# An LSTM's output weights loaded through the ring of the input weights, and its second block of steps fetched from inside the recurrence

## The chip, the core and the metric

The kernel runs on one core of a Trainium2 chip. Its engines are TensorE (PE in the profile; its weight loads are PEld), VectorE (DVE), ScalarE (ACT), GpSimd (POOL) and SyncE (SP, which here only issues DMAs and waits). The metric is the device time of one execution in microseconds; times before and after are medians of several runs. A "q" behind an engine's name in the profile means its instruction queue: the DMA issues and semaphore waits that the engine itself isn't busy with.

## The reference, cut to what matters

A stack of four graph layers and four other layers runs over 625 nodes with 512 features. The change lies in the sixth of these eight phases, a switching LSTM: the 625 nodes are 625 steps of one sequence, and at every step the argmax of four logits picks which of four sets of weights computes the gates.

```python
def step(carry, x_t):
    h, c = carry
    sel_in = jnp.concatenate([h, c, x_t], axis=-1)
    logits = sel_in @ W_sel.T + b_sel
    onehot = jax.nn.one_hot(jnp.argmax(logits, axis=-1), Sx, dtype=x_t.dtype)
    g_all = (jnp.einsum('bi,sgi->bsg', x_t, W_ih) + jnp.einsum('bh,sgh->bsg', h, W_hh)
             + b_ih + b_hh)
    g = jnp.einsum('bsg,bs->bg', g_all, onehot)
    h2, c2 = _lstm_activate(g, c)
    return ((h2, c2), h2)
```

`_lstm_activate` splits the gates into i, f, g and o and takes `c2 = sigmoid(f)*c + sigmoid(i)*tanh(g)` and `h2 = sigmoid(o)*tanh(c2)`. The result is added to the layer's input, and a normalized graph convolution follows.

## The kernel before, in words

Each phase is a function; `L2_ffn` is the LSTM. Everything outside the recurrence is written with a tile framework: a pool is a piece of on-chip memory that is taken from the left or the right end and given back when it is closed, a tile is a piece of a pool, and the framework works out all semaphores and the order on each engine's queue from what reads and writes what. A queue is worked off in order.

`L2_ffn` has two stages. In the first, the *input projection*, no step depends on another. Four experts times four gates make 16 turns (`turn = e * 4 + g`). Each turn takes a 512x512 block of W_ih, loaded by `C.weight` (line 91) into a ring of three 1 MB places (pool `weights`, at the right end), multiplies it with `xT`, the input laid out by feature (64 matmuls at line 1561, two halves of the nodes by four row blocks by four chunks of the sum), evacuates with a bias on ACT (line 1565) or DVE (lines 1568 and 1570) into a tile `gt`, and writes that to the DRAM tensor `gx` (line 1573), once for each half of the nodes. Two `gt` tiles take turns. In between, in the first twelve turns, half-megabyte pieces of W_hh come in as `raw` (issued by `load_whh`, line 1471; pool `e_raw`, two places, at the right end) and are split by ACT and DVE (`split`, lines 1478 to 1482) into three bf16 parts each, the tiles `wp`, which stay in memory. They are the recurrent weights of the gates i, f and g.

The second stage is the *recurrence*, 625 steps in which every engine runs its own hand-written program with its own semaphores (`tile_critical`, line 1674). Nothing in it begins before all that it uses is there; the framework makes SP wait for everything ahead of it and lets all engines go together. The fourth gate's recurrent weights stay in float32: four tiles `wo`, 8 KB a partition and 1 MB each, loaded through line 1471 after the projection's pools are closed; their pool `e2` lies in the room that `xT`, the `gt` tiles and their neighbours had. Behind `e2` lie the recurrence's own small tiles (pool `e_state`), among them two buffers `gxb` for 25 steps' worth of gx each (800 KB) and two `xsb` of the selection's input. `fetch(b)` loads one block of 25 steps into them (lines 1668 and 1670): `fetch(0)` and `fetch(1)` are issued ahead of the recurrence, and from block 2 on SP's own program in the recurrence issues them when DVE and ACT say that a buffer is free (line 1681); DVE and ACT wait for a block's arrival at its first step. The history `hist` of all h lies at the right end, where the ring of weights was.

In a step, TensorE multiplies the guessed expert's `wp` with h (line 1719) and `wo` (line 1748), DVE transposes and sums, ACT takes the functions. A matmul into `spare` (line 1760) opens each step's program on TensorE. The first instruction that DVE runs in the recurrence is the memset at line 1807.

Of the kernel before, what the change touches and what calls it, by code (L numbers as in the profile page):

```python
# [15 lines left out]
F32 = mybir.dt.float32  # L16
# [5 lines left out]
AF = mybir.ActivationFunctionType  # L22
# [6 lines left out]
N, D, P, NT = 625, 512, 125, 5  # L29
KC = D // 128  # L30
# [9 lines left out]
BLOCKS = N // STEPS  # L40
# [8 lines left out]
class Ctx:  # L49
# [21 lines left out]


    def open_mid(self, side):
        self.outer, self.inner = (self.stack.enter_context(ExitStack()) for _ in range(2))
        pool = lambda of, name, bufs: of.enter_context(self.tc.tile_pool(name=name + side, bufs=bufs, side=side))
        self.weights = pool(self.outer, "weights", 3)
        self.small = pool(self.outer, "small", 2)
        mid = pool(self.inner, "mid", 1)
        self.iota = mid.tile([128, N], F32, name="iota")
        self.nc.gpsimd.iota(self.iota, pattern=[[1, N]], base=0, channel_multiplier=0,  # L80
                            allow_small_or_imprecise_dtypes=True)
        self.x = mid.tile([P, NT, D], F32, name="x")
# [1359 lines left out]
def L2_ffn(C):  # L1442
# [6 lines left out]
    nc, tc, I = C.nc, C.tc, C.ins  # L1449
    S = 4  # L1450
    W = lambda name: I["L2_ffn_" + name]
    ORDER = (0, 1, 3, 2)
# [4 lines left out]
    with ExitStack() as st:  # L1457
        E = st.enter_context
# [3 lines left out]
        st1 = E(ExitStack())  # L1462
        pool = st1.enter_context(tc.tile_pool(name="e", bufs=1))
# [4 lines left out]
        def load_whh(dst, e, g, s0, n):  # L1468

            q = ORDER[g]  # L1470
            nc.sync.dma_start(dst, W("WhhT")[:, e, s0:s0 + n, q * D:(q + 1) * D])
# [12 lines left out]
        halves = [(e, g, s0) for e in range(S) for g in range(3) for s0 in (0, 2)]  # L1484

        with ExitStack() as st2:
            E2 = st2.enter_context
# [6 lines left out]
                C.normed(C.x)  # L1494
                C.feature_major(ps, xT, C.x)
            C.inner.close()
            st4 = E2(ExitStack())
            praw = st4.enter_context(tc.tile_pool(name="e_raw", bufs=2, side="right"))
            pgt = E2(tc.tile_pool(name="e_gt", bufs=2))
            st3 = E2(ExitStack())  # L1500
# [8 lines left out]
            b = praw.tile([64, 2, 128], F32, name="raw")  # L1509
# [34 lines left out]

            st3.close()
            ps = E2(tc.tile_pool(name="e_ps2", bufs=4, space=PSUM))
            for e in range(S):
                for g, q in enumerate(ORDER):
                    w = C.weight(W("WihT")[e, :, q * 512:(q + 1) * 512].rearrange("(k p) n -> p k n", p=128), KC)
                    turn = e * 4 + g  # L1550
                    pieces = []
                    for half in halves[turn * 2:turn * 2 + 2]:
                        raw = praw.tile([128, 2, D], F32, name="raw")
                        load_whh(raw, *half, 2)
                        pieces += [(raw, *half, s) for s in range(2)]
                    for n0, n in HALVES:
                        gt = pgt.tile([128, HALVES[0][1], 4], F32, name="gt")
                        for s in range(4):
                            pg = ps.tile([128, 512], F32, name="pg")
                            for k in range(KC):  # L1560
                                nc.tensor.matmul(pg[:, :n], w[:, k, s * 128:(s + 1) * 128], xT[:, k, n0:n0 + n],  # L1561
                                                 start=k == 0, stop=k == KC - 1)
                            c = (e * 4 + q) * 4 + s
                            if s % 2:
                                nc.scalar.activation(gt[:, :n, s], pg[:, :n], AF.Identity, scale=2.0 if g == 2 else 1.0,  # L1565
                                                     bias=(bias_2 if g == 2 else bias)[:, c:c + 1])
                            elif g == 2:
                                nc.vector.tensor_scalar(gt[:, :n, s], pg[:, :n], bias[:, c:c + 1], 2.0, op0=ALU.add, op1=ALU.mult)
                            else:
                                nc.vector.tensor_scalar(gt[:, :n, s], pg[:, :n], bias[:, c:c + 1], None, op0=ALU.add)  # L1570
                            if s % 2 and pieces:
                                split(*pieces.pop(0))
                        nc.sync.dma_start(gx[e, g, :, n0 * 4:(n0 + n) * 4], gt[:, :n].rearrange("p n c -> p (n c)"))

            st4.close()
            C.outer.close()
            held = E(tc.tile_pool(name="e_hist", bufs=1, side="right"))
            hist = held.tile([128, N + 1, KC], F32, name="hist")
            x4 = held.tile([P, D], F32, name="x4")
            nc.vector.tensor_copy(x4, kept[-1])  # L1580
            kept[-1] = x4
        pool = st1.enter_context(tc.tile_pool(name="e2", bufs=1))
        wo = [pool.tile([128, KC, D], F32, name=f"wo{e}") for e in range(S)]
        for e in range(S):
            load_whh(wo[e], e, 3, 0, KC)
        state = st1.enter_context(tc.tile_pool(name="e_state", bufs=1))
        with tc.tile_pool(name="e_ps3", bufs=1, space=PSUM) as ps:
            recurrence(C, state, ps, wp, wo, wsel, gx, xs, hist)
        st1.close()
        C.open_mid("left")  # L1590
        with tc.tile_pool(name="e_ps4", bufs=3, space=PSUM) as ps:
            for t in range(NT):
                pt = ps.tile([P, D], F32, name="pt")
                for s in range(KC):
                    nc.tensor.transpose(pt[:, s * 128:(s + 1) * 128], hist[:, 1 + t * P:1 + (t + 1) * P, s], C.ident)
                if t < NT - 1:
                    nc.scalar.copy(C.x[:, t], kept[t])
                    kept[t] = C.x[:, t]
                nc.vector.tensor_add(C.x[:, t], kept[t], pt)
                C.seen(t)  # L1600


def recurrence(C, pool, ps, wp, wo, wsel, gx, xs, hist):
# [19 lines left out]
    nc, tc = C.nc, C.tc  # L1623
    S, FIRST = 4, 6
# [17 lines left out]
    th = t_([128, 4], "th")  # L1642
# [20 lines left out]
    loaded = [nc.alloc_semaphore(f"lstm_dma{i}") for i in range(2)]  # L1663
    free = [[nc.alloc_semaphore(f"lstm_free_{k}{i}") for k in ("dve", "act")] for i in range(2)]

    def fetch(b):

        return (nc.sync.dma_start(gxb[b % 2].rearrange("p a u c -> p a (u c)"),
                                  gx[:, :, :, b * STEPS * 4:(b + 1) * STEPS * 4].rearrange("s q p f -> p (s q) f")),
                nc.sync.dma_start(xsb[b % 2], xs[0:1, b * STEPS * ROW:((b + 1) * STEPS + 1) * ROW]))  # L1670

    fetch(0)
    fetch(1)
    with tc.tile_critical():
        with nc.Block() as block:

            @block.sync
            def _(sync):
                for b in range(2, BLOCKS):
                    for f in free[b % 2]:  # L1680
                        sync.wait_ge(f, b // 2)
                    for d in fetch(b):
                        d.then_inc(loaded[b % 2], 16)

# [93 lines left out]
            @block.scalar  # L1778
            def _(act):
                for n in range(N):  # L1780
                    b, u = divmod(n, STEPS)
                    if b >= 2 and u == 0:
                        act.wait_ge(loaded[b % 2], 32 * (b // 2))
                    act.wait_ge(sem["ga0"], 1).then_inc(sem["ga0"], -1)  # L1784

                    act.copy(xrow[:, :S], xsb[b % 2][:, (u + 1) * ROW:(u + 1) * ROW + S]).then_inc(sem["x"])  # L1786
                    m = act.copy(hist[:, n], hT)
                    if u == STEPS - 1 and b < BLOCKS - 2:
                        m.then_inc(free[b % 2][1])
                    act.wait_ge(sem["ga"], 1)  # L1790
                    act.activation(act4[:, 0:3].rearrange("p g s -> p (g s)"), ga, AF.Tanh, scale=0.5).then_inc(sem["ifg"])  # L1791
                    act.wait_ge(sem["ao"], 1)
                    act.activation(so, go, AF.Sigmoid).then_inc(sem["so"])  # L1793
                    act.wait_ge(sem["c"], 1)
                    act.activation(th, c2, AF.Tanh, scale=0.5).then_inc(sem["th"])

            @block.vector
            def _(dve):
# [13 lines left out]
                dve.memset(hT, 0.0).then_inc(sem["hb"])  # L1812
                index()
                for b in range(BLOCKS):
                    if b >= 2:
                        dve.wait_ge(loaded[b % 2], 32 * (b // 2))
                    gxs = gxb[b % 2].rearrange("p (e g) u c -> p e g u c", e=S)
                    with dve.Fori(0, STEPS) as u:
                        wait("ix").then_inc(sem["dx"])
# [148 lines left out]


PHASES = [graph_and_L0_gnn, L0_ffn, L1_gnn, L1_ffn, L2_gnn, L2_ffn, L3_gnn, L3_ffn]  # L1970


# [48 lines left out]
```

## Time and profile before

| | us |
|---|---|
| median of three runs | 5129.65 (5128.46 to 5135.43) |
| the profiled execution | 5125.94 |
| its span, first to last instruction | 5123.2 |
| input projection, first to last matmul at line 1561 | 1366.0 to 1637.0 |
| first matmul of the recurrence | 1660.65 |
| last step's functions on ACT end | 4754.7 |
| a step of the recurrence, most frequent length | 4.6 |
| granted TensorE clock, mean over the span | 0.971 |

All times inside the execution count from the span's start. A row of the timeline gives the start, the length, the engine, the line, the operation with what it writes and reads, how often it came in a row, and in brackets how long its engine stood idle before it and what ended that. "issue" as the cause means that the profile shows nothing that the engine waited for. A row of the waits gives the total, the count and the longest wait. The chain of waits from the last instruction doesn't lead back through the recurrence here (it holds 8% of the span), so what follows is read from queues and windows. What can be seen apart from that is how much of the time DMAs carry: 246.84 MB over the whole span, 48 GB/s on the mean.

### The profile page before, as it was taken

What the parts mean: (1) busy time and instruction counts of PE and PEld (TensorE: products, weight loads), DVE (VectorE), ACT (ScalarE), POOL (GpSimd) and SP (SyncE); (2) the same over time, 40 slices, a digit from 0 to 9 for tenths busy, and PEclk for the clock granted to TensorE, in tenths of its full rate; (3) what the DMA queues carried; (4) which work ended last, traced back from release to release, by engine and by line L of the source; (5) the groups of instructions that cost most, each with busy time, mean ns of one, the idle gap of its engine ahead of it and who ended that gap; (6) DMA issues with size and microseconds to landing.
All of it is one profiled execution on the core that took longest, in us unless ns stands there. A gap on an engine that the chain in (4) does not pass through costs nothing. (4 is left out here: it accounts for less than half of the span.)

```text
span 5123.2 us, 184391 instructions
## 1 busy us (share of the span) xinstructions
PE 4752.5 (93%) x74110; PEld 3009.7 (59%) x74110; DVE 2662.2 (52%) x13487; ACT 1127.4 (22%) x4582; POOL 152.3 (3%) x140
## 2 busy tenths in 40 slices
PE   8998988799998999999999999999999999999988
PEld 6566746555575555555555555555555555555555
DVE  7533034400441566666656566665666656556258
ACT  8443112101341111111111111111111111111136
POOL 0000012100000000000000000000000000000011
PEclk9998998799999999999999999999999999999988
DMA  1133957211354000000000000000000000000200
GB/s 39 64 109 119 318 174 243 73 52 43 115 186 144 2 11 6 6 6 7 7 6 6 7 7 6 6 6 7 7 6 7 7 7 6 6 6 0 72 13 11
DMA packets 163039, 246.84 MB, mean 48 GB/s; under 512 B 67001, under 2 KB 67374, under 8 KB 162124
## 3 DMA queue, kind: packets, MB, share of 16 engines
q1 hardware_dynamic: 144480, 221.36, 13.2%
q0 software_dynamic: 8800, 16.92, 1.1%
q10 hardware_dynamic: 9594, 6.59, 0.5%
q8 instruction: 76, 1.25, 0.1%
q14 instruction: 89, 0.73, 0.0%
HBM read 198.90 MB, written 45.91 MB: 48 GB/s over the span
## 5 line engine op out<-in xcount | busy, mean ns | idle before, releaser
L1719 PE MATMUL pa<-wp,left 128*23 128x384 bf16 x33312 | 1495.6, 327 | 136.8 <-issue 46.6
L1719 PEld LDWEIGHTS pa<-wp,left 128*23 128x23 bf16 x33312 | 805.7, 93 | 649.6 <-DVE left L1856 154.0
L1748 PE MATMUL po<-wo,left 128*1 128x128 f32 x20000 | 655.7, 273 | 0.0
L1748 PEld LDWEIGHTS po<-wo,left 128*1 128x1 f32 x20000 | 481.1, 84 | 126.2 <-issue 0.2
L1760 PE MATMUL spare<-wo,ident 128*128 128x256 f32 x1250 | 437.4, 431 | 26.6 <-issue 26.6
L1824 DVE COPY col<-gxb 128x16 f32 x625 | 114.6, 183 | 654.3 <-DVEq L1799 654.3
L1834 DVE STREAM_TRANSPOSE col<-pa 128x384 f32<-128x384 f32 x625 | 349.5, 559 | 195.1 <-PE pa L1719 195.1
L1791 ACT ACTIVATE act<-ga 128x12 f32<-128x12 f32 x625 | 132.7, 212 | 1183.6 <-DVE ga L1836 1183.6
L1786 ACT COPY xrow<-xsb 1x4 f32<-1x4 f32 x625 | 120.5, 193 | 1214.8 <-ACTq L1784 1214.8
L1760 PEld LDWEIGHTS spare<-wo,ident 128*128 128x128 f32 x1250 | 186.1, 188 | 167.1 <-issue 167.1
L1561 PE MATMUL pg<-xT,w 128*128 128x312 f32 (+1 forms) x1024 | 270.4, 426 | 0.9 <-ACT gt L1565 0.5
L1561 PEld LDWEIGHTS pg<-xT,w 128*128 128x128 f32 x1024 | 193.2, 189 | 77.7 <-DVE gt L1570 1.1
L1711 PE MATMUL lg<-wso,th 128*1 128x8 f32 x5008 | 216.2, 169 | 14.0
L1707 PE MATMUL lg<-wsel,act 128*1 128x8 f32 x5008 | 216.2, 169 | 2.7 <-DVE act L1845 1.2
L1838 DVE STREAM_TRANSPOSE col<-po 128x128 f32<-128x128 f32 x625 | 198.2, 317 | 22.8
L1711 PEld LDWEIGHTS lg<-wso,th 128*1 128x1 f32 x5008 | 147.6, 81 | 73.5 <-DVE wso L1848 10.2
L509 PE MATMUL wide<-hot_dst,hot_src 125*125 125x512 bf16 x640 | 177.2, 390 | 12.9 <-DVE hot_dst L489 12.7
L1704 PEld LDWEIGHTS lg<-xrow,ones 1*1 1x1 f32 x1252 | 51.4, 76 | 232.9 <-issue 232.9
L1848 DVE TENSOR_TENSOR wso<-wsel,so 128x32 f32<-128x32 f32 x625 | 120.1, 192 | 115.3 <-ACT so L1793 114.4
L1707 PEld LDWEIGHTS lg<-wsel,act 128*1 128x1 f32 x5008 | 147.5, 81 | 50.4 <-DVE act L1845 4.9
L233 PE MATMUL po<-w,hT 128*125 128x512 f32 x400 | 175.1, 592 | 0.0
L1793 ACT ACTIVATE so<-go 128x4 f32<-128x4 f32 x625 | 128.3, 205 | 212.8 <-DVE go L1843 212.8
(506 smaller groups left out, 5867.7 us busy)
## 6 DMA issues: line engine op xcount, KB each, us to landing
ring<-in_L_ffn_W_dram SPq DMA_DIRECT2D x80, 1024.0 KB
gxb<-gx SPq DMA_DIRECT2D x25, 800.0 KB
w<-in_L_ffn_WihT_dram SPq DMA_DIRECT2D x16, 1024.0 KB
raw<-in_L_ffn_WhhT_dram SPq DMA_DIRECT2D x24, 512.0 KB
gx<-gt SPq DMA_DIRECT2D x16, 626.0 KB
made<-ys SPq DMA_DIRECT2D x39, 256.0 KB
gx<-gt SPq DMA_DIRECT2D x16, 624.0 KB
w<-in_L_gnn_Wl_dram SPq DMA_DIRECT2D x8, 1024.0 KB
```

The costliest lines, as they stand in the source:

```text
L233: self.nc.tensor.matmul(out, xT[:, k, t * P:(t + 1) * P], w[:, k, :], start=start and k == 0, stop=stop and k == k_n - 1)
L509: nc.tensor.matmul(wide[i], hs[:, k], hd[:, :W0], start=first, stop=last)
L1561: nc.tensor.matmul(pg[:, :n], w[:, k, s * 128:(s + 1) * 128], xT[:, k, n0:n0 + n], start=k == 0, stop=k == KC - 1)
L1707: pe.matmul(lg, c2[:, s:s + 1], wsel[:, 1, s], start=False, stop=False)
L1711: m = pe.matmul(lg, th[:, s:s + 1], wso[:, s], start=False, stop=s == KC - 1)
L1719: m = pe.matmul(pa[32 * j:32 * j + 2 * GAP + 1], upper[:, s], wp[e][:, s, i, j].rearrange("p g n -> p (g n)"), start=k == 0, stop=k == 11, ...
L1748: m = pe.matmul(po[32 * j:32 * j + 1].rearrange("p (u r) -> p u r", r=32), left[:, s, 0:1], wo[e][:, s].rearrange("p (u j r) -> p j u r", ...
L1760: pe.matmul(spare[:, :256], C.ident, wo[0][:, 0, :256], start=True, stop=True)
L1791: act.activation(act4[:, 0:3].rearrange("p g s -> p (g s)"), ga, AF.Tanh, scale=0.5).then_inc(sem["ifg"])
L1793: act.activation(so, go, AF.Sigmoid).then_inc(sem["so"])
L1834: dve.transpose(col[:, :12, :32], pa.rearrange("p (b r) -> p b r", r=32)).then_inc(sem["ta"])
L1838: dve.transpose(col[:, 12:, :32], po.rearrange("p (s r) -> p s r", r=32)).then_inc(sem["to"])
```

## The change

- The `small` pool gets its own stack and is closed before the projection, together with the pool of `x`; the pool of raw pieces takes the room.
- A function `load` keeps a list `ahead` of what the ring has been given. Load number 0 goes ahead of the loop, and turn t asks for all loads up to number t + 2, behind its pieces of W_hh. Numbers 0 to 15 are the input weights, 16 to 18 the output weights of experts 0 to 2, in the same ring.
- After the last turn with pieces of W_hh (turn 11) the pool of raw pieces is closed, and the output weights of expert 3 are loaded into a pool `e_wo` in its room.
- The weights' pool stays open to the end of `L2_ffn`. The pool `e2` is gone; `e_state` begins where the pools of the projection lay. `hist` gets a pool of its own, at the right end.
- `fetch(1)` is issued by SP's program in the recurrence, without a wait ahead of it; DVE and ACT wait for block 1 as they do for the later blocks, with the counts moved by one.
- One element of `th` is put through Tanh on ACT ahead of the recurrence.

```diff
     def open_mid(self, side):
-        self.outer, self.inner = (self.stack.enter_context(ExitStack()) for _ in range(2))
+        self.outer, self.smalls, self.inner = (self.stack.enter_context(ExitStack()) for _ in range(3))
         self.weights = pool(self.outer, "weights", 3)
-        self.small = pool(self.outer, "small", 2)
+        self.small = pool(self.smalls, "small", 2)
...
             C.inner.close()
-            st4 = E2(ExitStack())
+            C.smalls.close()
+            st4 = E(ExitStack())
             praw = st4.enter_context(tc.tile_pool(name="e_raw", bufs=2, side="right"))
...
+            ahead, wo = [], [None] * S
+
+            def load(upto):
+                while len(ahead) < upto:
+                    turn = len(ahead)
+                    if turn < 4 * S:
+                        q = ORDER[turn % 4]
+                        ahead.append(C.weight(W("WihT")[turn // 4, :, q * 512:(q + 1) * 512].rearrange("(k p) n -> p k n", p=128), KC))
+                    else:
+                        e = turn - 4 * S
+                        wo[e] = C.weights.tile([128, 2048], F32, name="w").rearrange("p (k n) -> p k n", k=KC)
+                        load_whh(wo[e], e, 3, 0, KC)
+                        ahead.append(None)
+
+            load(1)
             for e in range(S):
                 for g, q in enumerate(ORDER):
-                    w = C.weight(W("WihT")[e, :, q * 512:(q + 1) * 512].rearrange("(k p) n -> p k n", p=128), KC)
                     turn = e * 4 + g
+                    w = ahead[turn]
                     pieces = []
                     for half in halves[turn * 2:turn * 2 + 2]:
                         raw = praw.tile([128, 2, D], F32, name="raw")
                         load_whh(raw, *half, 2)
                         pieces += [(raw, *half, s) for s in range(2)]
+                    load(turn + 3)
...
-            st4.close()
-            C.outer.close()
+                    if len(halves) == 2 * turn + 2:
+                        st4.close()
+                        last = E(tc.tile_pool(name="e_wo", bufs=1, side="right"))
+                        wo[3] = last.tile([128, KC, D], F32, name="wo3")
+                        load_whh(wo[3], 3, 3, 0, KC)
+
+            load(4 * S + 3)
+            outer = C.outer
             held = E(tc.tile_pool(name="e_hist", bufs=1, side="right"))
-            hist = held.tile([128, N + 1, KC], F32, name="hist")
...
-        pool = st1.enter_context(tc.tile_pool(name="e2", bufs=1))
-        wo = [pool.tile([128, KC, D], F32, name=f"wo{e}") for e in range(S)]
-        for e in range(S):
-            load_whh(wo[e], e, 3, 0, KC)
+        hist = E(tc.tile_pool(name="e_hist2", bufs=1, side="right")).tile([128, N + 1, KC], F32, name="hist")
         state = st1.enter_context(tc.tile_pool(name="e_state", bufs=1))
...
+    outer.close()
...
     fetch(0)
-    fetch(1)
+
+    nc.scalar.activation(th[0:1, 0:1], C.ones[0:1, 0:1], AF.Tanh)
     with tc.tile_critical():
...
-                for b in range(2, BLOCKS):
-                    for f in free[b % 2]:
-                        sync.wait_ge(f, b // 2)
+                for b in range(1, BLOCKS):
+                    if b >= 2:
+                        for f in free[b % 2]:
+                            sync.wait_ge(f, b // 2)
                     for d in fetch(b):
                         d.then_inc(loaded[b % 2], 16)
...
-                    if b >= 2 and u == 0:
-                        act.wait_ge(loaded[b % 2], 32 * (b // 2))
+                    if b and not u:
+                        act.wait_ge(loaded[b % 2], 32 * ((b + 1) // 2))
...
-                    if b >= 2:
-                        dve.wait_ge(loaded[b % 2], 32 * (b // 2))
+                    if b:
+                        dve.wait_ge(loaded[b % 2], 32 * ((b + 1) // 2))
```

## The prediction

> **What bounds the kernel now.** I read the page first, then the stretch around the change: the table of windows, the queue of SP with its waits, the timeline, and last the DMA traffic. The page shows TensorE at work for 93% of the span, most of it in the recurrence, which the change leaves alone but for its first instructions:
>
> ```profile
> PE 4752.5 (93%) x74110; PEld 3009.7 (59%) x74110; DVE 2662.2 (52%) x13487; ACT 1127.4 (22%) x4582; POOL 152.3 (3%) x140
> L1561 PE MATMUL pg<-xT,w 128*128 128x312 f32 (+1 forms) x1024 | 270.4, 426 | 0.9 <-ACT gt L1565 0.5
> ```
>
> The second line is the input projection. Its 1024 matmuls are busy 270.4 us and idle 0.9 us in all: no weight load is waited for there. The windows show where time is free:
>
> ```profile
> 1600.00:1637.00 37.00, 37.00 (x141) 26.27 (x139) 7.01 (x9) 6.62 (x9) 0.00 (x0) 1.00 0.17 69
> 1637.00:1660.00 23.00, 0.03 (x1) 0.00 (x0) 1.13 (x7) 0.81 (x1) 0.00 (x0) 0.58 0.86 281
> ```
>
> (columns: length; PE, PEld, DVE, ACT, POOL busy with counts; TensorE's clock; DMA share; GB/s.) Up to 1637 us PE is full; then for 23 us only DMAs run. This is the only place from which the change can take much. SP's queue (start, length, engine, line, transfer) shows what fills it:
>
> ```profile
> 1637.06 0.37 SPq L1668 DMA_DIRECT2D gxb<-gx  x1
> 1637.90 1.20 SPq L1573 DMA_DIRECT2D gx<-gt  x1
> 1639.15 0.28 SPq L1670 DMA_DIRECT2D xsb<-xs  x1
> 1639.48 0.38 SPq L1668 DMA_DIRECT2D gxb<-gx  x1
> 1643.63 3.65 SPq L1471 DMA_DIRECT2D wo<-in_L_ffn_WhhT_dram  x4
> 1647.33 0.62 SPq L1670 DMA_DIRECT2D xsb<-xs  x1
> ```
>
> SP's waits (total, times, longest) and the recurrence's first instruction in the timeline show what each step stood behind:
>
> ```profile
> SPq L1674 <- DMA wo<-in_L_ffn_WhhT_dram: 10.8, 1, 10.8
> ...
> SPq L1668 <- PE pg L1561: 4.6, 1, 4.6
> SPq L1471 <- DMA gx<-gt: 3.6, 1, 3.6
> ...
> 1660.38 0.07 DVE L1807 MEMSET gi<- 1x8 f32 x1 [21.77 <-issue]
> ```
>
> The four output weights (1 MB each) are issued at 1643.63, when the last write of gx has landed (the wait of 3.6 us). The recurrence's gate, L1674, waits 10.8 us for them and opens about 1659.35; its first instruction runs at 1660.38, 1.03 us on. Note who waits for what: the fetch gxb waited for the last projection matmul, and the first wo load for the last gx write, though wo0 (8 KB a partition) fits in the room of xT (10 KB) alone. A tile of a new pool seems to wait until the whole old pools under its pool are free. I carry this into the new layout.
>
> **What the skill says.** The Trainium skill, DMA: Bandwidth & Descriptors, Specifications, puts line rate at transfers of 512 B and up. The trace agrees: gxb (2011 packets below 512 B) moves at about 318 GB/s, gx at about 420. ScalarE: Activation LUTs, What ACT_TABLE_LOAD costs, gives 1283 ns per load; the trace has 1.28 us. TensorE: Matmul & The Clock Gate, Part 1, has the clock fall to half when the array idles; here it reads 0.50 from 1641 to 1664 us and 1.00 from 1666. A gap of 13 us still contains that fall, so I take no gain from a warmer start.
>
> **Loads two turns ahead: 0.** SP issues input weights in this kernel at 1552.89, 1569.73 and 1586.56, each when a turn of 16.85 us ends; sixteen loads, the last at 1586.56 for the turn that starts near 1620. They are two turns ahead already, as a ring of three allows. If the new order lost that cover, one load would show about 5 us (1 MB issued at 1468.44, last traffic near 1472.9).
>
> **Output weights earlier.** wo3 goes into room freed by the raw tiles, whose last load is at 1461.69; wo0 and wo1 take the ring's places after turns 13 and 14, near 1602 and 1619. These three lie beside the projection, where DMA is at 0.43 or less after 1500; as PE idles 0.9 us with the same traffic of 1 MB each turn, cost 0. But wo2 takes the place of the last input weight and can't be issued before the last matmul, at 1637.06. So one load of 1 MB stays in the gap, ahead of the last gx write in SP's queue (that is ready at 1637.90, when ACT's last evacuation ends).
>
> The trace has the same pair, 1 MB load then gx write 0.85 us later:
>
> ```profile
> 1569.73 0.38 SPq L91 DMA_DIRECT2D w<-in_L_ffn_WihT_dram  x1
> 1570.58 0.32 SPq L1573 DMA_DIRECT2D gx<-gt  x1
> ...
> GB/s 0 0 0 0 0 0 0 90 25 82 49 74 295 369 360 360 262 319 287 279 221 238 311 415 464 445 388 439 459 260 200 60 0 0 0 0 0 0 0 0
> ```
>
> (window 1569 to 1579, slices of 0.25 us.) Traffic ends near 1576.9: 7.1 us from the first issue. So the last write ends near 1637.06 + 7.1 = 1644.15. For the write before it, issued at 1629.5, traffic ended at 1631.9 and SP woke at 1632.43: 0.55 us for the receipt. Landed: 1644.7, about 1 us later than now, since wo2 stands before it in place of the smaller gxb.
>
> **The fetches.** State tiles (gxb, xsb, left, th and so on; some 17.5 KB a partition) move down into the room of xT, x4 and the small tiles (12.9 KB) and the first gt (5 KB). By the reading above the first fetch then waits for that last gx write, where now it goes at 1637.06. This is the wait that takes the place of the one removed. Queued behind it on SP is only xsb; behind them the gate. Bounds: 0 if tiles wait one by one, 7.6 us (1644.7 less 1637.06) if pools wait whole; I take the latter. A lone fetch of this size:
>
> ```profile
> 1790.93 0.38 SPq L1668 DMA_DIRECT2D gxb<-gx  x1
> ...
> GB/s 272 278 317 320 326 307 323 323 326 307 323 323 317 278 294 212 146 54 10 0 0 0 0 0 0 0 0 0 0 0 0 0 0 0 0 0 0 0 0 0
> ```
>
> (window 1793 to 1798, slices of 0.125 us.) It ends near 1795.35, 4.4 us from issue. In the gap: 1644.7 + 4.4 = 1649.1; receipt 0.55 to 0.9 (0.9 from the end of traffic near 1658.45 to 1659.35 now), taken 0.7: 1649.8. xsb is 0.8 KB and lands with it. With the gate's 1.03, the recurrence starts near 1650.8 and not 1660.38: **9.6 us less**.
>
> fetch(1) leaves the gap and is issued by the block's SP at its start; step 25 needs it some 125 us later (fetches stand at 1790.93, 1914.90, 2038.46), and it takes 5. The waits on ACT and DVE at step 25 are then met: 0. Were they not, every engine of the chain would stop there, once.
>
> **Small parts.** DVE's six memsets of state (1637.46 to 1638.6, 0.9 us) now come after 1644.7 too and end before 1646, covered by the fetch. The one-element Tanh with its table load (1.28 us) also ends before 1647. It moves the load at 1664.12, which already ends 1 us before ACT's input arrives (1666.42); the Sigmoid's at 1666.68 is on the path (so comes at 1667.98, go was ready at 1667.0) and stays, since that set comes after. Gain 0; at most 0.9 if the load went too. Closing the small pool early and holding the weights' pool through the recurrence add no instruction; the tail after 4755 us is untouched.
>
> **Sum.** 0 - 9.6 + 0. The profiled execution took 5125.94 us, its span being 5123.2; the sum makes 5116.3. The median of the three runs is 3.7 us above the profiled one; the same amount off it: 5120.05, so 5120.0.
>
> **Rivals.** *B, the fetch is not held* (tiles wait one by one), or the gx write goes before wo2. Three transfers of 2.5 MB then overlap. At 300 to 330 GB/s, as now in this gap, with 1.0 us to first traffic: ended near 1646, gate near 1647.5; gain 12.9, so 5116.8. For it: gxb now goes ahead of the last write. Against: the two waits quoted.
>
> *C, the change does little of what it says*: the three ring loads come only after the last turn. Then 3 MB stand before the gx write: at 385 GB/s, the rate of the four loads now, two more loads add 5.4 us; gain 4.2, so 5125.4. Against: the ring now loads punctually.
>
> *D, slower: each step of the recurrence costs more* since wo and the state lie elsewhere in memory and the loops elsewhere in the program. 9.6 / 625 = 15 ns a step eats the gain, from there on it is slower, and 32 ns (20 us) is slower by 0.2%; taken at 50 ns: 5120.0 + 31 = 5151. Against: 459 of the 625 steps now last 4.6 us, through 25 copies of the vector loop in different places of the program, so place isn't worth much there. For it: nothing but that any small loss counts 625 times.
>
> **How the numbers follow.** My case A (9.6) gets 0.58, B 0.24, C 0.07, D 0.11. A's own range is 5116.5 to 5123: receipt and traffic 1 us each way, runs of before spread over 7 us. 0.2% is 10.26 us (about what a measurement of this kernel can tell from no change), so the bound runs through A: 0.38 of A is beyond it. Faster: 0.22 + nearly all of B 0.23 = 0.45. Within: the rest of A 0.36, B 0.01, C 0.07 = 0.44. Slower: D, 0.11. The range reaches from B's far side, 5115, to just past C, 5126; D is left out.
>
> **What would show it.** In SP's queue: three wo loads before 1637, one at 1637.06, the gx write at 1637.90, gxb near 1644.7 and one fetch only before the gate. PE's idle time before L1760 falls from 23.6 to about 14 us; L1561 idles as now; steps stay at 4.6 us. Wrong: gxb issued near 1637 (B), two wo loads after 1637 (C), a longer mean step or PE idle in the projection (D).

## The result, and the profile after

The changed kernel takes 5122.12 us (median of 19 runs, 5106.89 to 5133.79), the kernel before beside it 5132.30 us (19 runs, 5122.89 to 5141.70). The ratio is 0.9977, with a 95% interval of 0.9970 to 0.9984: 8 to 15 us less. The forecast was 9.6 us less, at 5120.0 us.

The profiled execution took 5123.18 us, its span being 5121.3. Against the profiled execution of before (5125.94, shorter than 18 of its 19 timed runs) that is only 2.8 us, so a comparison of the two spans would have misled. The stretch around the change has to be read by itself. First the windows (length; PE, PEld, DVE, ACT, POOL busy; TensorE's clock; DMA share; GB/s), up to the last projection matmul and from there to the recurrence:

```profile
1600.00:1638.46 38.46, 38.43 (x147) 27.28 (x145) 7.01 (x9) 7.37 (x9) 0.00 (x0) 1.00 0.37 122
1638.46:1652.44 13.98, 0.00 (x0) 0.00 (x0) 0.70 (x7) 2.29 (x3) 0.00 (x0) 0.60 0.64 179
```

The empty stretch is 13.98 us long; before it ran from 1637.06 to 1660.38, 23.32 us. So 9.34 us have gone, and the projection stays full while it carries three more loads, two of them in this window (0.37 of the DMA time where it was 0.17). Its row in the page's list of groups confirms that nothing waits there:

```profile
L1580 PE MATMUL pg<-xT,w 128*128 128x312 f32 (+1 forms) x1024 | 271.4, 428 | 0.3 <-DVE sel L1539 0.3
```

SP's queue in the timeline shows what was moved out and what is left:

```profile
1604.80 0.38 SPq L1471 DMA_DIRECT2D w<-in_L_ffn_WhhT_dram  x1
...
1621.63 0.38 SPq L1471 DMA_DIRECT2D w<-in_L_ffn_WhhT_dram  x1
...
1638.46 0.38 SPq L1471 DMA_DIRECT2D w<-in_L_ffn_WhhT_dram  x1
1639.30 0.32 SPq L1592 DMA_DIRECT2D gx<-gt  x1
1646.55 0.37 SPq L1689 DMA_DIRECT2D gxb<-gx  x1
1646.97 1.17 SPq L1691 DMA_DIRECT2D xsb<-xs  x1
1652.39 0.38 SPq L1689 DMA_DIRECT2D gxb<-gx  x1
```

wo0 and wo1 come in the ring's turns, wo3 went at 1471.58; wo2 can only go when the last matmul has ended, and the last write of gx stands behind it. The fetch of the first block waits for that write. The last line is the fetch of the second block, now issued by the recurrence itself. SP's waits (total, times, longest) say the same:

```profile
SPq L1471 <- PE pg L1580: 21.5, 3, 7.2
...
SPq L1689 <- DMA gx<-gt: 6.7, 1, 6.7
...
SPq L1696 <- DMA gxb<-gx: 2.6, 1, 2.6
```

The gate (now L1696) no longer waits 10.8 us for output weights, but 2.6 us for the fetch. In the place of the removed wait stand 6.7 us for gx, as the prediction's case A had it.

What the stretch gave doesn't all arrive. In windows of 2 us (length, PE busy, TensorE's clock, DMA share, GB/s) the first steps before the change are:

```profile
1660.00:1662.00 2.00, 1.34 (x8) 0.50 0.03 8
1662.00:1664.00 2.00, 2.00 (x40) 0.50 0.00 0
1664.00:1666.00 2.00, 2.00 (x59) 0.86 0.00 0
1666.00:1668.00 2.00, 0.39 (x16) 1.00 0.03 8
1668.00:1670.00 2.00, 0.69 (x2) 1.00 0.04 8
```

and after it:

```profile
1656.00:1658.00 2.00, 2.00 (x32) 0.50 0.30 62
1658.00:1660.00 2.00, 1.33 (x40) 0.90 0.04 8
1660.00:1662.00 2.00, 0.00 (x0) 0.95 0.00 0
1662.00:1664.00 2.00, 1.34 (x7) 0.50 0.04 8
1664.00:1666.00 2.00, 2.00 (x41) 0.50 0.00 0
1666.00:1668.00 2.00, 2.00 (x32) 0.50 0.00 0
```

Before, the clock rises within the first step and stays, though PE stands still for 2.9 us between the two steps. After, it rises at the end of the first step, PE stands still for 3.3 us between the steps, and the second step runs at half clock again. From the first memset to the second step's gates on ACT it takes 16.84 us in place of 13.54. The same program doesn't always start like this; the experiments come back to it.

### The profile page after: what moved, and what is told of

Same layout as the page of the kernel before. It is cut to its first block, busy times and chain, and to the rows that moved or that the text cites. A ratio compares the mean times of both kernels' runs of the same rounds, so it can differ in the third digit from the quotient of the medians.

```text
span 5121.3 us, 184400 instructions
## 1 busy us (share of the span) xinstructions
PE 4776.7 (93%) x74110; PEld 3015.0 (59%) x74110; DVE 2663.2 (52%) x13487; ACT 1129.5 (22%) x4583; POOL 152.4 (3%) x140
## 5 line engine op out<-in xcount | busy, mean ns | idle before, releaser
L1771 PE MATMUL po<-w,left 128*1 128x128 f32 x14752 | 484.3, 273 | 0.0
L1783 PE MATMUL spare<-w,ident 128*128 128x256 f32 x1250 | 437.9, 432 | 17.6 <-issue 17.6
L1771 PEld LDWEIGHTS po<-w,left 128*1 128x1 f32 x14752 | 352.1, 84 | 97.3 <-issue 0.3
L1783 PEld LDWEIGHTS spare<-w,ident 128*128 128x128 f32 x1250 | 186.2, 188 | 158.2 <-issue 158.2
L1734 PE MATMUL lg<-wso,th 128*1 128x8 f32 x5008 | 216.2, 169 | 13.1
L1771 PE MATMUL po<-wo,left 128*1 128x128 f32 x5248 | 177.1, 273 | 0.0
```

What stands on the lines that cost most here:

```text
L1734: m = pe.matmul(lg, th[:, s:s + 1], wso[:, s], start=False, stop=s == KC - 1)
L1771: m = pe.matmul(po[32 * j:32 * j + 1].rearrange("p (u r) -> p u r", r=32), left[:, s, 0:1], wo[e][:, s].rearrange("p (u j r) -> p j u r", ...
L1783: pe.matmul(spare[:, :256], C.ident, wo[0][:, 0, :256], start=True, stop=True)
```

## The experiments

All intervals are 95% intervals of the ratio to the kernel before, run on the same chip. "Stretch" is the time from the last projection matmul to the first memset of the recurrence, "second gate" and "eleventh gate" the time from that memset to ACT's first function of step 2 and of step 11. "Half clock" is the part of the time to the second gate in which the granted clock was 0.50. "Rest" runs from the eleventh gate to the last step's functions, "tail" from there to the end of the span; "sum" is stretch, eleventh gate and rest together. The profiles gave (us):

| kernel | stretch | half clock | second gate | eleventh gate | rest | sum | tail | ratio |
|---|---|---|---|---|---|---|---|---|
| before | 23.3 | 4.2 | 13.5 | 61.3 | 3032.2 | 3116.8 | 369.3 | |
| after | 14.0 | 12.8 | 16.8 | 65.8 | 3028.6 | 3108.4 | 374.5 | 0.9977 (0.9970 to 0.9984) |
| e7, after again | 13.9 | 8.1 | 15.1 | 64.1 | 3029.9 | 3107.9 | 367.7 | 0.9980 (0.9972 to 0.9988) |
| e1, fetch(1) back | 17.2 | 7.4 | 14.3 | 63.6 | 3027.7 | 3108.5 | 375.5 | 0.9999 (0.9989 to 1.0008) |
| e8, the same again | 17.2 | 9.9 | 15.5 | 63.4 | 3030.4 | 3111.0 | 372.0 | 0.9972 (0.9961 to 0.9983) |
| e5, only fetch(1) moved | 21.0 | 4.7 | 13.7 | 61.5 | 3031.7 | 3114.2 | 377.1 | 1.0005 (0.9997 to 1.0013) |
| e9, the same again | 21.2 | 7.4 | 14.8 | 63.6 | 3032.0 | 3116.8 | 374.1 | 0.9993 (0.9984 to 1.0003) |
| e2, loads in their own turn, no Tanh | 14.0 | 13.1 | 17.1 | 66.2 | 3027.7 | 3107.9 | 374.9 | 0.9990 (0.9983 to 0.9997) |
| e3, first fetch early | 8.9 | 12.5 | 16.4 | 65.3 | 3028.0 | 3102.2 | 374.9 | 0.9969 (0.9957 to 0.9981) |
| e4, warm matmuls | 13.8 | 3.4 | 13.4 | 64.6 | 3021.7 | 3100.1 | 377.4 | 0.9983 (0.9977 to 0.9990) |
| e6, combined | 9.2 | 10.2 | 15.7 | 73.8 | 3023.6 | 3106.6 | 373.5 | 0.9970 (0.9959 to 0.9981) |
| e10, early fetch and Sigmoid | 8.8 | 4.9 | 14.1 | 61.5 | 3030.7 | 3101.0 | 371.6 | 0.9966 (0.9953 to 0.9979) |

The stretch repeats to within 0.2 us for the same kernel; the tail, which no version touches, is 367.7 and 374.5 us for the very same program (after and e7). That is why each part is judged by the stretch first.

e1 to e4 ran on one chip, e5 to e7 on a second, e8 to e10 on a third. The medians of the kernel before differ between them (5125.21, 5132.35 and 5135.77 us; 5132.30 beside the changed kernel), while the changed kernel (5122.12 and 5122.07) and e2, which stands for it on the first of these chips (5120.77; its two edits prove to be worth nothing), hardly do. So a ratio from e1 to e4 lies higher than the same gain would give elsewhere; why the kernel before is quicker on that chip, no run shows. Kernels on one chip can be compared directly: on the mean e1 is 5.8 us slower than e2 (95%: 3.2 either way), e3 7.6 us faster (3.0), e4 2.7 us faster (2.8), and e6 is 5.2 us faster than e7 (4.7).

What the second gate follows is the half clock. Windows from the first memset to the second gate (length, PE busy, clock, DMA share, GB/s), of after and e7, which are one program, then of e3 and e10, whose stretches are equally long:

```profile
1652.44:1669.28 16.84, 13.21 (x200) 0.62 0.22 52
1654.28:1669.41 15.13, 11.42 (x196) 0.73 0.24 57
1649.11:1665.55 16.44, 13.08 (x200) 0.62 0.22 53
1655.13:1669.18 14.05, 10.51 (x201) 0.83 0.26 62
```

A mean clock of 0.62 over 16.84 us is 2 * 0.38 * 16.84 = 12.8 us at half clock. Put in order by that column, from 3.4 to 13.1, the second gates of all twelve profiles stand in order too, from 13.4 to 17.1. The length of the stretch doesn't decide it (e3 and e10), nor does the program (after and e7).

**e1: fetch(1) alone goes back ahead of the recurrence.**

```diff
     fetch(0)
+    fetch(1)
...
-                for b in range(1, BLOCKS):
-                    if b >= 2:
-                        for f in free[b % 2]:
-                            sync.wait_ge(f, b // 2)
+                for b in range(2, BLOCKS):
+                    for f in free[b % 2]:
+                        sync.wait_ge(f, b // 2)
...
```

> The changed kernel with one part undone: the fetch of block 1 stands ahead of the recurrence again. Theory (the gain is the shorter gap, and what is left of the gap is a chain of transfers): 0.8 MB more behind the first fetch, at about 315 GB/s, so the gap from the end of the last projection matmul to the recurrence's first memset grows from 14.0 to about 16.6 us, and the time by about 2.6 us. Rival (the fetch of block 1 is hidden, only the output weights counted): gap 14.0 as in the changed kernel.

The stretch is 17.22 us, 3.24 more than after: the second fetch lies behind the first one on the wire and the gate waits for both. That is the price of this part, 0.6 us above the expected growth. The timed ratio, 0.9999, lay higher than the price explains beside the 0.9977 of the whole, which was measured on another chip; beside e2, on the same chip, the 5.8 us (3.2 either way) hold the price.

**e5: the other half alone.** The kernel before with only this move:

```diff
     fetch(0)
-    fetch(1)
...
-                for b in range(2, BLOCKS):
-                    for f in free[b % 2]:
-                        sync.wait_ge(f, b // 2)
+                for b in range(1, BLOCKS):
+                    if b >= 2:
+                        for f in free[b % 2]:
+                            sync.wait_ge(f, b // 2)
...
```

> The kernel before with one part of the change alone: the second block of steps is asked for by the recurrence's own program, and wo[3] stays where it was, behind the last projection matmul. Theory (the parts add up): the 3.24 us that the stretch between last projection matmul and first recurrence memset grew by in e1_fetch1_back come off here too, so 23.3 becomes 20.1 (20.7 by the prediction's own working); the time is 2.6 to 3.2 us below before, ratio 0.9994 to 0.9995, which is at the edge of what the runs resolve. Rival (the two parts overlap): the stretch stays above 22, because the gate's last issue is not what starts the engines. For the cold steps: if a stretch of about 20 us leaves the clock in the phase that 17 and 23 us left it in, the second gate of the recurrence comes 13.5 to 14.3 us after the memset; if the phase is chance, it may come anywhere from 13 to 17.

The stretch falls by 2.3 us, to 21.0, less than the 3.24 expected; the time doesn't fall (1.0005). So the two halves, each alone, had shown nothing, and the whole 10 us. Both were run again:

> The kernel of e1_fetch1_back once more, unaltered, beside that of e5_fetch1_only, since the two halves alone measured nothing (0.9999 and 1.0005) while the whole measured 0.998. Theory (the halves add up, and the two ratios were at the unlucky end of their intervals): the stretch is 17.2 us again, 6.1 less than before, and the ratio 0.9982 to 0.9992. Rival (the whole is worth more than its halves, by something that the stretch does not show): the ratio stays at 0.9995 or above.

> The kernel of e5_fetch1_only once more, unaltered. Theory (additive): stretch 21.0 us, 2.35 less than before, ratio 0.9991 to 0.9999. Rival (the whole is worth more than its halves): 1.0003 or above again. What the stages before the projection and the attention behind the recurrence take in the profile differs from the first profile of the same kernel by some us, either way.

The stretches came out at 17.2 and 21.2 us. The ratios moved: 0.9999 became 0.9972, which lies below the expected range, and 1.0005 became 0.9993. The two intervals of one and the same kernel (0.9989 to 1.0008 and 0.9961 to 0.9983) don't meet. The second was taken on another chip, so what is due to the chip and what to the time isn't told apart; either way an interval from one chip says less than it seems to. Averaged over both, the halves stand at 0.9986 and 0.9999, 1.5 thousandths together, beside 2.0 and 2.3 for the whole. The rival (the whole is worth more than its halves) loses what spoke for it, but these times can't exclude a difference of 3 us. The stretches nearly add up: 6.1 and 2.2 us (mean of 2.3 and 2.1) make 8.3, beside 9.4 for the whole. The other 1.1 us come of both together, since the move of fetch(1) is worth 3.24 us in the new arrangement and 2.2 in the old.

**e2: the loads asked for in their own turn, and no Tanh ahead.**

```diff
-            load(1)
             for e in range(S):
                 for g, q in enumerate(ORDER):
                     turn = e * 4 + g
+                    load(turn + 1)
...
-                    load(turn + 3)
...
-    nc.scalar.activation(th[0:1, 0:1], C.ones[0:1, 0:1], AF.Tanh)
```

> The changed kernel with two parts undone: each input weight is asked for in its own turn (the ring still takes the output weights after the last turn's), and the one-element Tanh is left out. Theory: both are worth nothing; the ring's loads still go out when a turn ends, projection idle time stays below 1 us, gap 14.0 within 0.5, and the first step's Tanh load is hidden. Rival (the order of the loads is part of the gain): PE idle in the projection of 5 us or more, or output weights after the last matmul and a gap near 19.

SP's queue in this kernel:

```profile
1592.90 0.38 SPq L91 DMA_DIRECT2D w<-in_L_ffn_WihT_dram  x1
...
1609.73 0.38 SPq L1471 DMA_DIRECT2D w<-in_L_ffn_WhhT_dram  x1
...
1626.56 0.38 SPq L1471 DMA_DIRECT2D w<-in_L_ffn_WhhT_dram  x1
```

The loads stand where a ring place comes free, 16.83 us apart, whichever line asks for them; the projection idles 0.3 us and the stretch is 13.97. The first step's Tanh load ends at 1662.34, before ACT's input at 1664.21. Both parts are worth nothing by the trace. The ratio, 0.9990, was taken on the chip where all ratios are higher; its interval just touches that of the whole.

**e3: the first fetch gets room of its own**, so that it no longer waits for the gt tiles to be given back. `gxb[0]` and `xsb[0]` move to the right end, behind wo3, the fetch is asked for ahead of wo2, and the pool of the gt tiles is closed by itself behind wo2 (not shown):

```diff
                         load_whh(wo[3], 3, 3, 0, KC)
+                        first = E(tc.tile_pool(name="e_first", bufs=1, side="right"))
+                        gxb0 = first.tile([128, S * 4, STEPS, 4], F32, name="gxb0")
+                        xsb0 = first.tile([1, (STEPS + 1) * ROW], F32, name="xsb0")
...
+            nc.sync.dma_start(gxb0.rearrange("p a u c -> p a (u c)"), gx[:, :, :, :STEPS * 4].rearrange("s q p f -> p (s q) f"))
+            nc.sync.dma_start(xsb0, xs[0:1, :(STEPS + 1) * ROW])
             load(4 * S + 3)
...
-    fetch(0)
```

> The changed kernel with the first block's buffers (gxb0, xsb0) in a pool of their own, in room that no tile of the projection holds late, and its fetch asked for as soon as the last first-half write of gx has landed. Theory (the fetch is held by whole pools below it): gxb goes out before the last matmul ends; the gap is then one 1 MB load and one gx write, 9.0 to 9.8 us; time 4 to 5 us below the changed kernel, 5117. Rival (the fetch hides beside the load anyway, or shares its bandwidth): gap 12 or more.

SP's queue, and in the second fence its wait at the gate:

```profile
1635.69 0.37 SPq L1603 DMA_DIRECT2D gxb<-gx  x1
1641.10 0.32 SPq L1593 DMA_DIRECT2D gx<-gt  x1
1641.51 0.39 SPq L1471 DMA_DIRECT2D w<-in_L_ffn_WhhT_dram  x1
```

```profile
SPq L1701 <- DMA w<-in_L_ffn_WhhT_dram: 2.6, 1, 2.6
```

The fetch goes 4.5 us before the last matmul ends, ahead of the last write of gx: it needs nothing from that write, and held back it was only by its place. (That it is asked for earlier in the program isn't what freed it: in the kernel before it was asked for behind that write, and went ahead of it.) The stretch falls to 8.9 us, the ratio to 0.9969. What ends it now is wo2, which here goes 1.3 us after the last matmul, behind the gx write. wo2 ahead of that write, or with a place of its own, wasn't tried.

**e4: matmuls behind the projection to keep the clock up**, 48 of them on constants, whose result is not used. (A float32 matmul shows as two in the profile, these as 96; the 64 matmuls of a turn are 32 in the program.)

```diff
             load(4 * S + 3)
+            hot = ps.tile([128, 512], F32, name="pg")
+            for _ in range(WARM):
+                nc.tensor.matmul(hot[:, :128], C.ident, C.ones, start=True, stop=True)
```

> The changed kernel with 48 matmuls of 128x128 on the identity after the last projection matmul, whose result nobody reads: TensorE stays at work for about 10 of the 14 us of the gap. Theory (the changed kernel gave back some 3 us in its first two steps, which ran at half clock): gap 14.0, clock 1.0 at the first step, second step's gates on ACT 13 us after the recurrence's first memset, where the changed kernel's profile has 16.8; time 3 us below. Rival (cold start is the same in both and costs nothing that matters): 16 to 17 us as before and no gain.

They do what they should at the start: the second gate comes after 13.37 us, not 16.84. But the eleventh comes after 64.6: from the third gate to the fourth (step 2 in the expectations, which count from 0) it takes 14.41 us, where it is 10.1 to 11.4 in all kernels without them. The clock is full at the first instruction (1658.26), falls soon after and rises again within the first step:

```profile
1656.00:1658.00 2.00, 0.00 (x0) 1.00 0.23 46
1658.00:1660.00 2.00, 1.55 (x28) 0.72 0.32 73
1660.00:1662.00 2.00, 2.00 (x32) 0.50 1.23 306
1662.00:1664.00 2.00, 1.94 (x56) 0.93 0.19 40
```

There is a gain that nobody had expected: the rest is 3021.7 us, some 6 us less than in e2 or e3. It lies in the steps that last longer than 5.2 us, 137 from the eleventh on. They take 825.5 us here and 825.6 in e6, the other kernel with such matmuls, and 832.4 to 833.7 in all ten other profiles; 34 of them are shorter by 0.1 to 0.3 us each. So the sum is the lowest of all, 7.8 us below that of e2; the times on the same chip show 2.7 us of it (2.8 either way). Why those steps are shorter, and whether such matmuls pay, stays open.

**e6: early fetch, 28 warm matmuls, and Sigmoid in place of Tanh ahead of the recurrence.** Of the edit only the last part is shown:

```diff
-    nc.scalar.activation(th[0:1, 0:1], C.ones[0:1, 0:1], AF.Tanh)
+    nc.scalar.activation(th[0:1, 0:1], C.ones[0:1, 0:1], AF.Sigmoid)
```

> Early first fetch and the warm matmuls together (28 of them, about 6 us, behind the last projection matmul), with Sigmoid's table asked for ahead of the recurrence in place of Tanh's. Theory (gap, cold steps and table load are three separate terms): the stretch from the last projection matmul to the first memset is 8.8 to 9.4 us as in e3_early_fetch, the second gate comes 12.3 to 13.0 us after the memset (13.4 in e4_warm less the table load's share, about 1 us, if no load remains inside the first step), the time is 8 to 9 us below the kernel after, ratio to before 0.9950 to 0.9965. Rival (the clock gate hands back what it granted): the steps after the first two run colder instead, and the ratio stays at e3_early_fetch's 0.997. Second rival (Sigmoid's set does not hold Tanh): a load of 1.28 us shows inside the first step as before, and the second gate comes at 13.4 or later.

The stretch is 9.2 us as expected; the second gate, expected after 12.3 to 13.0 us, comes after 15.7, and the ratio stops at 0.9970. Up to the eleventh gate the clock is at half for 23.9 us, where it is 19.4 in e3, as the rival had it, and PE stands still more often. Beside e3 the eleven steps lose 8.5 us, and the rest gives back 4.4. PE's rows in the timeline, with its idle time in brackets:

```profile
1671.80 0.19 PE L1735 MATMUL lg<-xrow,ones 1*1 1x8 f32 x2 [3.40 <-issue]
...
1677.45 4.03 PE L1750 MATMUL pa<-wp,left 128*23 128x384 bf16 x48 [3.53 <-issue]
...
1697.00 1.22 PE L1791 MATMUL spare<-w,ident 128*128 128x256 f32 x2 [4.63 <-issue]
```

In each of the three, PE stands in the middle of its program with nothing to wait for. The DMA view of the same stretches shows what else happens there; for 1692 to 1697:

```profile
q8 instruction: 1, 0.02, 2.3%
```

One packet on a queue that carries instructions (the columns are packets, MB and share). Between the third gate and the fourth e3 has one such hole, of 3.38 us, where e6 has two, the first two rows above; the third row makes e6's way from the sixth gate to the seventh 9.99 us long in place of 4.60. The hole between the first two steps looks the same: in all twelve profiles it lasts 2.75 to 3.41 us, and one 16 KB packet of this kind starts 2.8 to 3.3 us before PE goes on. More instructions on TensorE's queue go with other and more holes; that the packets are what PE waits for is likely, but no run isolates it.

**e10: the same without the warm matmuls.**

> The early first fetch of e3_early_fetch and Sigmoid's table asked for ahead of the recurrence, without the warm matmuls. Theory (the warm matmuls of e6_combined took back what the rest gave, through the two long early steps of 14.55 and 9.99 us that shifted instruction fetches brought): the stretch is 8.9 us, no table load inside the first step, step 2 is about 11 us and step 5 4.6 us, and the eleventh gate comes 63.5 to 65.5 us after the memset (65.3 in e3_early_fetch, 73.8 in e6_combined); ratio 0.9960 to 0.9970. Rival (the cold start eats the table load's share too, since the clock's fall decides): eleventh gate at 65.3 or later, ratio as e3_early_fetch, 0.997.

ACT's rows in the timeline:

```profile
1651.21 1.28 ACT L1700 ACT_TABLE_LOAD   x1 [4.02 <-DVE x L1610]
...
1661.57 0.21 ACT L1819 ACTIVATE act<-ga 128x12 f32<-128x12 f32 x1 [2.65 <-DVE ga L1864]
1662.14 0.20 ACT L1821 ACTIVATE so<-go 128x4 f32<-128x4 f32 x1 [0.36 <-DVE go L1871]
```

One load, ahead of the recurrence, serves both functions. From the first gates to `so` it is 0.57 us; after the change it was 1.52 (1659.34 to 1660.86). The Trainium skill, ScalarE: Activation LUTs, Table sets: the hidden batching unit, lists Tanh in Sigmoid's set; these rows agree. The eleventh gate comes after 61.5 us, earlier than the range I gave, because here the clock didn't fall between the first steps. The ratio, 0.9966, is the lowest of all, but its interval holds those of e3 and e6 for the most part. By their ratios the three are one group, some 5 us below the changed kernel, and the stretch lost 5 us; the comparisons on one chip (e3 with e2, e6 with e7) say 7.6 and 5.2 us, with intervals that hold 5.

**e7: the changed kernel once more.**

> The changed kernel itself, unaltered, beside the others on this chip. The stretch is 14.0 us as in its first profile. If the two cold first steps come with a stretch of that length, the second gate comes 16.4 to 17.1 us after the memset again; if they are chance, another value from 13.4 up is as likely. Ratio to before 0.997 to 0.9985.

The ratio repeats (0.9980), the stretch too (13.9), the second gate doesn't: 15.13 us. The attention behind the recurrence doesn't either. Fifty microseconds of it in the windows, first of after, then of e7, the same program (both begin 171 us before the end of the span):

```profile
4950.00:5000.00 50.00, 45.49 (x209) 30.10 (x211) 42.17 (x93) 35.08 (x75) 9.10 (x6) 0.66 0.00 1
```

```profile
4945.00:4995.00 50.00, 41.84 (x209) 27.68 (x208) 41.97 (x92) 33.50 (x73) 8.56 (x6) 0.80 0.00 1
```

209 matmul records each time, at a mean clock of 0.66 and of 0.80; the tails differ by 6.8 us.

## Why the prediction was right

- **Loads two turns ahead, 0.** Right. e2 undoes it and SP issues the loads at the same distance.
- **Output weights earlier, with wo2 and the gx write left in the gap.** Right to the issue: wo2 goes with the end of the last matmul (1638.46), gx 0.84 us after it, as in the pair that was taken as the model. That pair's traffic lasted 7.1 us, which from 1638.46 gives 1645.56; here the last of it ended near 1646.0, and SP issued the fetch at 1646.55, so it was the traffic that took some 0.4 us longer, and the receipt took the 0.55 us assumed. (The ring's places come free when a turn ends, 1603.4 and 1620.3 by the issues that I quoted, and not near 1602 and 1619; wo0 and wo1 went at 1604.80 and 1621.63, in a projection that began 1.0 us later.) With wo2 alone behind the last matmul, rival C is out.
- **The first fetch held by the room it stands in.** Right, and the rival B (not held) is out: the fetch waited 6.7 us for gx. DVE's first memsets of left, act, xrow and gl, other tiles of the same pool, waited for the same write and ran at 1646.49 to 1646.61; that fits pools that wait whole, though no view shows which tile lies where. e3 shows that with another place the fetch starts before the last matmul ends. From the fetch's issue to the first memset it took 5.89 us, against 6.1 in the sum (4.4, 0.7 and 1.03).
- **fetch(1) hidden.** Right: it is issued at 1652.39, lands under the first steps, and the first step that needs it has its gates at 1790.06, 4.62 us after those before it. e1 prices it at 3.24 us in this arrangement, e5 and e9 at 2.3 and 2.1 in the old one.
- **Tanh, 0.** Right: from the first gates to `so` it is 1.52 us after, 1.53 before. The bound of 0.9 us for the case in which no load is left inside the step is about right too: e10 measures 0.95.
- **D, dearer steps.** Out: the short steps (under 5 us) from the eleventh on average 4.604 us after and 4.608 before; for one kernel (e1 and e8) they were 4.602 and 4.606. The rest is even shorter, by 3.6 us after and, between kernels without warm matmuls on one chip, by 1.3 to 1.8 us wherever the output weights lie in the ring (e7 beside e5; e8 and e10 beside e9); no run shows why.
- **The sum.** The stretch shrank by 9.34 us where 9.6 were forecast. The absolute time came out 2.1 us above the forecast, and the larger sample of the kernel before, with a median of 5132.30 and not 5129.65, covers that. That the time agrees as well as the stretch does is luck in part: the first eleven steps took 4.5 us more than before (2.8 in e7) and the rest 3.6 less (2.3). The prediction had both at nothing, and they nearly cancel; the sum fell by 8.4 us (8.9 in e7).
- **The step that was too simple: "I take no gain from a warmer start".** The clock does fall in the shorter gap too, and no gain came. But I read the cold start as one fall of equal cost. There are two chances to fall: in the gap, and again in the hole of some 3 us between the first two steps. What it costs is the time at half clock up to the second gate, which was 4.2 us before and 12.8 after, but 8.1 in e7; the spread for one program is 16.8 and 15.1, 13.7 and 14.8, 14.3 and 15.5 us to the second gate. The length of the hole doesn't decide either: in e8 the clock fell with one of 2.75 us, in e10 it stayed with one of 3.17. The Trainium skill, TensorE: Matmul & The Clock Gate, Part 1, describes a free-running window of about 3.4 us, so that the same kernel starts differently from run to run; the traces agree: from the projection's end to the eleventh gate, in all twelve, each stretch of one clock that begins there and ends there lasts 3.41 us or a multiple of it. That the place of the steps in these windows decides how many of them are cold is the reading that fits; no run sets that place.

## What to carry to other kernels

When a transfer seems to wait for data, ask whether it waits for room: which pool lies beneath its tile, and who gives that back last. Here a place for the first block that comes free earlier took a further 5.1 us from the stretch, with the same transfers. A few microseconds gained in one place are shown by the stretch itself, which repeats to 0.2 us, and by times of both kernels on one chip, better on more than one; neither the span of one profile nor one timed interval shows them.

## What was not expected of the hardware

- The 19 runs of the changed kernel spread over 27 us (5106.89 to 5133.79), and its mean clock with it (0.973 to 0.966). The profiles place part of this in the attention: tails of 367.7 and 374.5 us for the same instructions.
- Extra matmuls in an idle stretch change steps far behind them, though nothing waits for them: with 48 of them the way from the third gate to the fourth was longer by about 3.4 us, with 28 (and the other two edits) by 3.5, and from the sixth to the seventh by 5.4; with either number 34 later steps were shorter by 0.1 to 0.3 us each, some 7 us in all. They also left TensorE warm at the first instruction, and within the first two steps it was at half clock for 3.4 us (e4) and 10.2 us (e6).
